# Exponentials of a pair attention, moved from ScalarE's table to a power on GpSimd

## The chip, the cores and the metric

The kernel runs on one core of a Trainium2 chip. The metric is the device time of one execution in microseconds (us). The engines of a core are named as in the profile: PE is TensorE (matmuls; PEld are its weight loads), DVE is VectorE, ACT is ScalarE, POOL is GpSimd, SP is SyncE, which here issues DMAs. Each engine takes its instructions in order.

## The reference

Two layers on x of 4 x 1024 x 256 in float32: a recurrent attention and a mixture of experts, then a pair attention and a feed-forward net with two hidden layers. The change lies in the pair attention alone. Cut to what matters, it computes for each batch:

```
q = X @ Wq.T ; k = X @ Wk.T ; Vy = X @ Wy_w.T + Wy_b      # 64 features a
e[i,j,a]    = relu(signed_sqrt(q[i,a] + k[j,a]))
scores[i,j] = sum_a e[i,j,a] * Wphi[a]
ex          = exp(scores - max_j scores)
denom       = sum_j ex
part1       = ex @ Vy
Ew[i,a]     = sum_j ex[i,j] * e[i,j,a]
out         = (part1 + Ew @ We_w.T + We_b * denom) / (denom + 1e-9)
```

The table e has 1024 x 1024 x 64 entries per batch, and it is used twice: for the scores, and, once the exponentials are known, for Ew.

## The kernel before

The first stage (to about 1300 us) is the first layer. The second stage runs the pair attention of all four batches, and interleaves with it the rest of the first layer (`first_rest`), the preparation of the next batch (`prepare`) and the feed-forward net (`dense`), cut into pieces that one function, `work(room)`, emits at fixed points. A list of allowances, `ROOM`, says how much of it goes in at each point. A few feed-forward pieces run on after the last block.

The pair attention is cut into blocks of 32 query rows, `NB` = 32 blocks a batch and 128 in all (class `Block`). A block has eight steps, each with one pair of tiles. The two halves of a pair tile (128 partitions, which hold 16 queries by 8 features, by 1024 keys) go through the same work:

- `pair` (L1313, L1315, L1316): adds the query to the spread keys and clips at zero, six of sixteen halves on ACT (L1313), ten on DVE (L1315); ACT takes the square root of the whole pair (L1316), and PE sums the features into the scores (L1320, PSUM tile `sc`).
- `top` (L1330 to L1333): DVE takes the maximum of each of the 128 rows of scores; a row of queries lies over four partitions, so a small matmul brings their maxima together.
- `exps` (L1337 to L1340): DVE takes the final maximum with its sign turned (`neg`); ACT makes `ex` from the scores, 128 x 256. At its end `switch()` emits a Silu or Gelu of the feed-forward net (L1290), if one is due, so that ACT's tables are changed at one place in a block.
- `spread` (L1345), twice a block: PE copies the exponentials of half of the queries to the partitions where the pair tiles have them (`xb`, in PSUM, 128 x 1024).
- `weigh` (L1364): DVE multiplies each half tile by `xb` and sums over the keys, 16 times a block.
- `turn` and `turned` (L1350, L1354): PE transposes `ex`, and ACT copies it out for the product with the values. `finish` (L1412 among its lines) completes four blocks at a time.

The order of the work is written out by hand in a loop over blocks n and steps p. At each step it weighs pair p of block n, emits some of the other work, and makes a pair that is 11 or 12 pairs ahead, as the ring of `RING` = 12 pair tiles allows. At p = 5 it emits `top` of block n + 1, and at p = 6 its `exps` and its first `spread`; the second `spread` follows at p = 0 of its own block. What DVE is given between `neg` and the first `weigh` that reads the new `xb` is thus the making of pairs at steps 6 and 7, the weighing of step 7 and pieces of the other work. On POOL there are only additions in this stage: `finish` (L1412), `dense` (L1278) and `first_rest` (L1095, L1165).

Of the kernel before, what the change touches and what calls it, by code (L numbers as in the profile page):

```python
# [7 lines left out]
F32 = mybir.dt.float32  # L8
AF = mybir.ActivationFunctionType
ALU = mybir.AluOpType  # L10
# [4 lines left out]
P = 128  # L15
# [7 lines left out]
CAP = 640.0  # L23
EPS_RHO = 1e-8
EPS_DEN = 1e-9
DFF = 1024
FB = 256
U = 512
# [12 lines left out]
@with_exitstack  # L41
def block_kernel(ctx: ExitStack, tc: tile.TileContext, a, out):
    nc = tc.nc
    keep = ctx.enter_context(tc.tile_pool(name="keep", bufs=1))


    kept = ctx.enter_context(tc.tile_pool(name="kept", bufs=1, space=DRAM))
    link = {
        "x1": [kept.tile([U, C], F32, tag=f"x1_{j}", name=f"x1_{j}") for j in range(B * T // U)],
        "x2": [kept.tile([FB, C], F32, tag=f"x2_{j}", name=f"x2_{j}") for j in range(B * T // FB)],  # L50
        "gates": [kept.tile([1, 2, B, C], F32, tag=f"gates{j}", name=f"gates{j}") for j in range(2)],
        "brow": kept.tile([1, C], F32, tag="brow", name="brow"),
        "yg": kept.tile([P, 4, U], F32, tag="yg", name="yg"),
        "qd": kept.tile([T, 64], F32, tag="qd0", name="qd0"),
        "kd": kept.tile([8, P, T], F32, tag="kd0", name="kd0"),
        "vd": kept.tile([T, C], F32, tag="vd0", name="vd0"),
    }

    ident = keep.tile([P, P], F32, tag="ident", name="ident")
    nc.scalar.dma_start(ident, a["ident"])  # L60
    eps = keep.tile([P, 3], F32, tag="eps", name="eps")
    for i, v in enumerate((EPS_LN, EPS_GN, EPS_RHO)):
        nc.vector.memset(eps[:, i : i + 1], v)
    cols = [keep.tile([P, 6, 2, B], F32, tag=f"mcols{i}", name=f"mcols{i}") for i in range(2)]
    seen = keep.tile([P, NE], F32, tag="seen", name="seen")
    nc.gpsimd.memset(seen, 0.0)
    first_layer(tc, a, link, cols, seen, ident, eps)
    pair_attention(tc, a, link, out, cols, seen, ident, eps)
# [733 lines left out]
def pair_attention(tc, a, link, out, cols_of, seen, ident, eps):  # L802
# [10 lines left out]
    nc = tc.nc  # L813
# [4 lines left out]
    with tc.tile_pool(name="at_w", bufs=1) as wp, tc.tile_pool(name="at_2", bufs=2) as p2, tc.tile_pool(  # L818
        name="at_k", bufs=1
    ) as pk, tc.tile_pool(name="at_s", bufs=RING) as ring, tc.tile_pool(  # L820
        name="at_d", bufs=2, space=DRAM
    ) as dr, tc.tile_pool(name="at_f", bufs=1) as pf, tc.tile_pool(name="at_fw", bufs=4) as pfw, tc.tile_pool(
        name="at_sc", bufs=2, space=PSUM
    ) as psc, tc.tile_pool(name="at_xb", bufs=2, space=PSUM) as pxb, tc.tile_pool(
        name="at_g", bufs=2, space=PSUM
# [10 lines left out]
        nc.vector.memset(wsel, 0.0)  # L836
        for g in range(8):
            nc.vector.tensor_scalar_mul(wsel[:, g, 16:32], query, phi[:, g : g + 1])
        same = wp.tile([P, P], F32, tag="same", name="same")
        part = wp.tile([P, 4], F32, tag="part", name="part")  # L840
        pick = wp.tile([P, 4, 2, P], F32, tag="pick", name="pick")
# [155 lines left out]
        def weights(j, i):  # L997
            for k in range(j * ALL + i, min(j * ALL + i + 3, B * T // FB * ALL)):
                if k not in held:
                    held[k] = pfw.tile([P, DFF], F32, tag="fw", name="fw")  # L1000
                    nc.sync.dma_start(held[k], a["ffw"][k % ALL * P : (k % ALL + 1) * P, :])
# [23 lines left out]
        def first_rest():  # L1025
# [6 lines left out]
            nc.sync.dma_start(x, a["x"][(NU - 1) * U :, :].rearrange("(t p) c -> p t c", p=P))  # L1032
            fw = [pfw.tile([P, DFF], F32, tag="fw", name="fw") for i in range(3)]
            wo, (center, avg, tri, ones) = fw[0][:, 0:512], (fw[0][:, 512 + P * i : 640 + P * i] for i in range(4))
# [113 lines left out]
            def half(n):  # L1148
                t = pfw.tile([P, DFF], F32, tag="fw", name="wd").rearrange("p (k n) -> p k n", k=2)
                i, k = divmod(n, 2)  # L1150
                nc.sync.dma_start(t, w_down[:, 2 * k : 2 * k + 2, 2 * i * C : 2 * (i + 1) * C])
                return t
# [141 lines left out]
        def switch():  # L1294
            while waiting:
                waiting.pop(0)()

        class Block:
# [36 lines left out]
            def exps(self):  # L1335
                self.neg = p2.tile([P, 1], F32, tag="neg", name="neg")
                nc.vector.tensor_reduce(self.neg, self.sc[:, 256:260], AX.X, ALU.max, negate=True)  # L1337
                self.ex = p2.tile([P, 256], F32, tag="ex", name="ex")
                nc.scalar.activation(self.ex, self.sc[:, 0:256], AF.Exp, bias=self.neg)  # L1339
                switch()  # L1340

            def spread(self, s):
# [25 lines left out]
        def finish(n, ew, exT):  # L1368
# [37 lines left out]
            den = p2.tile([P, 1], F32, tag="den", name="den")  # L1406
            nc.vector.tensor_scalar_add(den, o[:, C : C + 1], EPS_DEN)
            nc.vector.reciprocal(den, den)
# [120 lines left out]
def _arranged(inputs):  # L1529
# [21 lines left out]
    for n in "vg":  # L1551
# [13 lines left out]
    arr["ffw"] = np.concatenate(  # L1565
        [w[n].reshape(2, P, 2, 512).transpose(2, 1, 0, 3).reshape(2 * P, DFF) for n in ("w1", "w2")]
        + [w[n].reshape(8, P, 8, P).transpose(2, 1, 0, 3).reshape(8 * P, DFF) for n in ("h1", "h2")]
        + [w["w3"].reshape(2, 4, P, C).transpose(0, 2, 1, 3).reshape(2 * P, DFF)]
    )
# [21 lines left out]
```

## Time and profile before

| | |
|---|---|
| median of 3 runs | 5620.06 us (5608.47 to 5624.56) |
| the profiled execution's own time | 5612.39 us |
| its span, first to last instruction | 5610.4 us |
| mean granted TensorE clock | 0.884 |
| first and last exponential (L1339) | 1307.2 and 5386.9 us |
| ACT table loads at L1339 / L1316 / L1290 | 128 / 127 / 46, 1283 ns each |

The span is what the instruction records cover; the profiled execution's own time has about 2 us more around it. In the rows, a group of instructions shows busy time and the mean of one in ns; after the bar stand the idle time of its engine in front of it and what ended that. In the waits, each line has the engine and line that waited, what it waited for, the total in us, how many times, and the longest. In the timeline a line has a start in us, a duration, the engine and the instruction.

### The profile page before, as it was taken

What the parts mean: (1) busy time and instruction counts of PE and PEld (TensorE: products, weight loads), DVE (VectorE), ACT (ScalarE), POOL (GpSimd) and SP (SyncE); (2) the same over time, 40 slices, a digit from 0 to 9 for tenths busy, and PEclk for the clock granted to TensorE, in tenths of its full rate; (3) what the DMA queues carried; (4) which work ended last, traced back from release to release, by engine and by line L of the source; (5) the groups of instructions that cost most, each with busy time, mean ns of one, the idle gap of its engine ahead of it and who ended that gap; (6) DMA issues with size and microseconds to landing.
All of it is one profiled execution on the core that took longest, in us unless ns stands there. A gap on an engine that the chain in (4) does not pass through costs nothing.

```text
span 5610.4 us, 74442 instructions
## 1 busy us (share of the span) xinstructions
PE 4574.4 (82%) x28714; PEld 2695.6 (48%) x28714; DVE 4532.2 (81%) x7889; ACT 3854.0 (69%) x3550; POOL 534.3 (10%) x463
## 2 busy tenths in 40 slices
PE   6789888765778778888896788897888897888888
PEld 2233333332345445555463555564555564555566
DVE  5777777656888888889988788888889989898951
ACT  2322222117888888888887888888788888888840
POOL 3434433220000000000000000000000000000000
PEclk8789999886889889998898889898899898988999
DMA  4333333332011131211112221111211211111123
GB/s 133 100 94 94 95 89 97 102 95 68 25 36 47 38 70 61 82 61 57 45 69 46 60 82 59 51 63 34 71 53 60 87 65 44 57 56 50 44 95 115
DMA packets 223734, 385.48 MB, mean 69 GB/s; under 512 B 69346, under 2 KB 114963, under 8 KB 222995
## 3 DMA queue, kind: packets, MB, share of 16 engines
q1 hardware_dynamic: 211890, 378.46, 21.7%
q8 instruction: 226, 3.70, 0.3%
q10 hardware_dynamic: 11488, 2.25, 0.2%
q14 instruction: 130, 1.06, 0.1%
HBM read 340.74 MB, written 39.86 MB: 68 GB/s over the span
## 4 chain that ended last, share of the span: by engine, by line
PE 44%; DVE 31%; ACT 16%; SPq 4%; issue 3%; DMA 2%; POOL 0%; ACTq 0%; DVEq 0%; POOLq 0%
PE ff_ps L1249 14%; DVE s L1364 13%; PE sc L1320 8%; ACT s L1316 7%; DVE s L1315 5%; PE e_ps L591 5%; PE xb L1345 4%; DVE state L777 2%; ACT s L1313 2%; PE ff_ps L1226 2%; PE out_ps L1268 2%; ACT wide L1290 2%; ACT L1316 2%; DVE pr L779 2%; SPq L955 1%
## 5 line engine op out<-in xcount | busy, mean ns | idle before, releaser
L1364 DVE CUSTOM_DVE_ANT_0 s<-s,xb 128x1024 f32<-128x1024 f32 x2048 | 2412.6, 1215 | 37.7 <-PE xb L1345 36.5
L1316 ACT ACTIVATE s<-s,eps 128x2048 f32<-128x2048 f32 x1024 | 2039.0, 2001 | 379.3 <-DVE s L1315 362.3
L1320 PE MATMUL sc<-s,wsel 128*32 128x256 f32 x16384 | 1235.4, 427 | 727.2 <-ACT s L1316 725.8
L1320 PEld LDWEIGHTS sc<-s,wsel 128*32 128x32 f32 x16384 | 463.3, 117 | 1334.5 <-ACT s L1316 898.6
L1249 PE MATMUL ff_ps<-wide,fw 128*128 128x256 f32 x4096 | 983.5, 389 | 8.6 <-ACT wide L1290 8.5
L1315 DVE TENSOR_SCALAR s<-kB,qt 128x1024 f32<-128x1024 f32 x1280 | 947.3, 758 | 35.3 <-DMA wk<-in_Wk_dram 17.1
L1313 ACT ACTIVATE s<-kB,qt 128x1024 f32<-128x1024 f32 x768 | 875.0, 1139 | 102.7 <-DMA wk<-in_Wk_dram 59.1
L1249 PEld LDWEIGHTS ff_ps<-wide,fw 128*128 128x128 f32 x4096 | 769.2, 193 | 181.9 <-issue 74.5
L1345 PE MATMUL xb<-ex,pick 128*128 128x256 f32 x2048 | 591.6, 439 | 16.6 <-ACT ex L1339 15.8
L1345 PEld LDWEIGHTS xb<-ex,pick 128*128 128x128 f32 x2048 | 423.3, 218 | 208.1 <-issue 75.5
L591 PE MATMUL e_ps<-wd,hid 128*128 128x512 f32 x896 | 424.7, 621 | 0.0
L709 POOL TENSOR_TENSOR kv<-vb,out_k 128x512 f32<-128x512 f32 x256 | 323.7, 1272 | 332.4 <-DVE state L777 202.7
L777 DVE TENSOR_TENSOR_SCAN state<-dec,carry,kv 128x512 f32<-128x512 f32 x256 | 326.0, 1273 | 9.6 <-POOL carry L772 5.0
L1412 POOL TENSOR_TENSOR xr<-xr,fin 128x256 f32<-128x256 f32 x32 | 34.2, 1068 | 2877.8 <-DVE fin L1410 2650.4
L591 PEld LDWEIGHTS e_ps<-wd,hid 128*128 128x128 f32 x896 | 174.8, 201 | 245.0 <-issue 238.4
L779 DVE TENSOR_TENSOR pr<-state,rec 128x512 f32<-128x512 f32 x256 | 176.0, 687 | 110.8 <-ACT state L775 57.5
L1226 PE MATMUL ff_ps<-wide,fw 128*128 128x256 f32 x1024 | 255.5, 400 | 3.3 <-DVE wide L1213 1.5
L1238 DVE TENSOR_TENSOR wide<-ff_ps,ffn_s 128x512 f32<-128x512 f32 x128 | 88.1, 688 | 208.7 <-PE ff_ps L1249 207.7
L769 ACT COPY carry<-state 128x1 f32<-128x1 f32 x255 | 47.8, 188 | 271.4 <-DVE state L777 270.3
L1226 PEld LDWEIGHTS ff_ps<-wide,fw 128*128 128x128 f32 x1024 | 200.2, 201 | 50.1 <-issue 12.1
L1330 DVE TENSOR_REDUCE own<-sc 128x1 f32<-128x256 f32 x128 | 54.0, 422 | 170.6 <-PE sc L1320 170.6
L1364 DVE DVE_READ_ACCUMULATOR2_ANT ew<- 128x1 f32 x2048 | 168.7, 82 | 0.0
(247 smaller groups left out, 3879.9 us busy)
## 6 DMA issues: line engine op xcount, KB each, us to landing
fw<-in_ffw_dram SPq DMA_DIRECT2D x352, 512.0 KB
vb<-vd SPq DMA_DIRECT2D x1024, 64.0 KB
wd<-in_w_down_dram SPq DMA_DIRECT2D x28, 1024.0 KB
kB<-kd SPq DMA_DIRECT2D x32, 512.0 KB
kd<-wide SPq DMA_DIRECT2D x24, 512.0 KB
vd<-out_v SPq DMA_DIRECT2D x8, 512.0 KB
kd<-kn SPq DMA_DIRECT2D x16, 256.0 KB
vy<-vd SPq DMA_DIRECT2D x4, 1024.0 KB
```

The lines of the kernel that those rows point to most:

```text
L591: nc.tensor.matmul(ps, hid[:, k, t * P : (t + 1) * P], wd[:, k, :], start=k == 0, stop=k == HID // P - 1)
L709: nc.gpsimd.tensor_mul(kv, vb[:, g % 2, :], ready[u]["k"][:, n // HN, :])
L777: nc.vector.tensor_tensor_scan(s[:, 1 : U + 1], dec, kv, c, ALU.mult, ALU.add)
L779: nc.vector.tensor_mul(pr, s[:, 0:U], rec)
L1226: nc.tensor.matmul(ps[:, h, :], w[:, k, o : o + P], hT[:, k, :], start=k == 0, stop=k == 1)
L1249: nc.tensor.matmul(ps[:, h, :], w[:, k * P : (k + 1) * P], of[:, k, :], start=k == 0, stop=k == 7)
L1313: nc.scalar.activation(t[:, h, :], kB[self.b][g], AF.Relu, bias=q)
L1315: nc.vector.tensor_scalar(t[:, h, :], kB[self.b][g], q, 0.0, ALU.add, ALU.max)
L1316: nc.scalar.activation(t, t, AF.Sqrt, bias=eps_rho)
L1320: nc.tensor.matmul(self.sc[32 * j : 32 * j + 32, 0:256], wsel[:, g, 16 * (1 - s) : 16 * (1 - s) + 32], t[:, h, 256 * j : 256 * (j + 1)], s ...
L1345: nc.tensor.matmul(xb[:, 256 * j : 256 * (j + 1)], pick[:, j, s, :], self.ex, start=True, stop=True)
L1364: nc.vector.tensor_tensor_reduce(t[:, h, :], t[:, h, :], self.xb[s], 1.0, 0.0, ALU.mult, ALU.add, ew[:, self.n % 4, col : col + 1])
```

## The change

The new tile `euler` holds e, 2.718281828459045, once per partition, and is read as if it were 256 columns wide. ACT adds `neg` to the scores with Identity instead of Exp. GpSimd then computes euler to the power of `ex`, elementwise in float32, in place in `ex`. All readers of `ex` (both spreads and `turn`) take it from GpSimd now.

```diff
+EULER = 2.718281828459045
...
+        euler = wp.tile([P, 1], F32, tag="euler", name="euler")
+        nc.gpsimd.memset(euler, EULER)
+        euler = euler.to_broadcast([P, 256])
...
                 self.ex = p2.tile([P, 256], F32, tag="ex", name="ex")
-                nc.scalar.activation(self.ex, self.sc[:, 0:256], AF.Exp, bias=self.neg)
+                nc.scalar.activation(self.ex, self.sc[:, 0:256], AF.Identity, bias=self.neg)
+                nc.gpsimd.tensor_tensor(self.ex, euler, self.ex, ALU.pow)
                 switch()
```

## The prediction

> **What bounds the kernel now.** I read the page first (busy shares, slices, the chain), then the groups of instructions, the waits, and the timeline of one block.
>
> ```profile
> PE 4574.4 (82%) x28714; PEld 2695.6 (48%) x28714; DVE 4532.2 (81%) x7889; ACT 3854.0 (69%) x3550; POOL 534.3 (10%) x463
> ...
> POOL 3434433220000000000000000000000000000000
> ...
> PE 44%; DVE 31%; ACT 16%; SPq 4%; issue 3%; DMA 2%; POOL 0%; ACTq 0%; DVEq 0%; POOLq 0%
> PE ff_ps L1249 14%; DVE s L1364 13%; PE sc L1320 8%; ACT s L1316 7%; DVE s L1315 5%; PE e_ps L591 5%; PE xb L1345 4%; DVE state L777 2%; ACT s L1313 2%; PE ff_ps L1226 2%; PE out_ps L1268 2%; ACT wide L1290 2%; ACT L1316 2%; DVE pr L779 2%; SPq L955 1%
> ```
>
> The exponentials live in the stage from about 1304 to 5430 us. There POOL is idle (the zeros of its row from slice 11 on), while PE, DVE and ACT share the chain; a sum over that stage gives DVE 3602.75 us busy of 4126, ACT 3503.53, PE 3396.66. No engine bounds it alone; DVE comes nearest. In the chain, "ACT L1316" without a tile is table loads: 2%, about 112 us. Loads of L1339 are under the list's last 1%, so at most 56 us. The groups give the sizes:
>
> ```profile
> L1364 DVE CUSTOM_DVE_ANT_0 s<-s,xb 128x1024 f32<-128x1024 f32 x2048 | 2412.6, 1215 | 37.7 <-PE xb L1345 36.5 <-ACT wide L1290 0.4
> ...
> L1339 ACT ACT_TABLE_LOAD x128 | 164.2, 1283 | 2.3
> L1316 ACT ACT_TABLE_LOAD x127 | 162.9, 1283 | 3.8 <-DVE s L1315 1.5
> ...
> L1339 ACT ACTIVATE ex<-sc,neg 128x256 f32<-128x256 f32 x128 | 60.7, 474 | 24.1 <-DVE neg L1337 22.8
> ...
> L1412 POOL TENSOR_TENSOR xr<-xr,fin 128x256 f32<-128x256 f32 x32 | 34.2, 1068 | 2877.8 <-DVE fin L1410 2650.4 <-DMA xr<-x 186.8 <-DVE ln_rs L895 40.7
> ```
>
> The waits say what late ACT work costs the others:
>
> ```profile
> PE sc L1320 <- ACT s L1316: 685.3, 360, 25.9
> ...
> DVE own L1330 <- PE sc L1320: 170.6, 43, 31.0
> ...
> DVE s L1364 <- PE xb L1345: 36.5, 49, 2.3
> ```
>
> PE waits much for square roots, but only what reaches DVE counts: 170.6 us in front of the row maximum (L1330). Last, one block's exponential in the timeline (start, duration):
>
> ```profile
> 3027.42 0.16 DVE L1337 TENSOR_REDUCE neg<-sc 128x1 f32<-128x4 f32 x1 [1.34 <-PE sc L1333]
> 3027.43 1.28 ACT L1339 ACT_TABLE_LOAD   x1
> ...
> 3028.73 0.47 ACT L1339 ACTIVATE ex<-sc,neg 128x256 f32<-128x256 f32 x1
> ...
> 3030.15 1.99 PE L1345 MATMUL xb<-ex,pick 128*128 128x256 f32 x8
> ...
> 3030.56 1.42 DVE L1315 TENSOR_SCALAR s<-kB,qt 128x1024 f32<-128x1024 f32 x2
> ...
> 3032.18 1.22 DVE L1364 CUSTOM_DVE_ANT_0 s<-s,xb 128x1024 f32<-128x1024 f32 x1 [0.20 <-PE xb L1345]
> ```
>
> This is the place that decides. After `neg` DVE has work of its own until 3031.98, 4.40 us from neg's end at 3027.58; a block near 3055 gives 4.45. Then it needs `xb`, which needs `ex`. The two paths are even: the idle time on xb is only 36.5 us over 128 blocks, 0.29 us each.
>
> **The change, part by part.**
>
> Removed on ACT: L1339's 128 loads, 164.2 us, and the square root's reload after them. L1290 still loads for Silu or Gelu 46 times, directly after an exponential, and a reload follows each; so about 127 - 46 = 81 of L1316's loads go, 104 us. Together 268 us of ACT. That Identity needs no load is in the trace: L909, Identity, ran at 3004.48 between square roots at 3002.57 and 3006.55 with no load. What of the 268 is on the path? The chain allows 112 + 56 = 168 us at most, the wait at L1330 170.6; I take 170 as the whole gain there. A rule bears on this. A load shows 1.28 us, and the timeline has the activation 1.30 us after the load's start, with the square root in front ending at 3027.41. The Trainium skill, "ScalarE: Activation LUTs", What ACT_TABLE_LOAD costs, adds a drain for about 2.66 us in all. By it ACT would be freed of 209 x 2.66 = 556 us instead of 268. The rows decide: 268.
>
> Kept: one ACT pass of 0.474 us (L1339, now Identity; same form). The `euler` memset is once, 0.1 us like the other small POOL memsets, under the loads at the stage's start: nothing.
>
> Added: 128 POOL instructions, 128x256, one per block, each in series between ACT's subtraction and PE's L1345. Call its duration X. The trace shows no power. From below, the nearest row is L1412, an addition of the same shape: 0.73 us when undisturbed, 1.07 mean. [...]a power is a logarithm, a product and an exponential[...], so arithmetic, not reading, should set X and that row is only a floor. From above I use a price. The Trainium skill, "GPSIMD Engine Reference", Performance pitfalls for Q7 kernels, puts a chain of dependent fp32 operations at 4 cycles per element each, at the 1.2 GHz of its Specifications: 256 columns x 4 / 1.2 = 853 ns per step of the chain. How many steps is my assumption: ScalarE's exp is three multiply-adds over a finely cut table (first page named, Cubic eval); without the table I double that, six for the exponential, six for the logarithm, one product: 13 steps, 11.1 us, and 0.2 us fixed (POOL additions of 1024 and 512 columns, 2348 and 1272 ns, extrapolate to 0.2): X = 11.3 us. With independent chains interleaved it could be near 3 us; with twice the steps and range handling near 30. I keep 0.73 as the lower end and 30 as the upper end of this form.
>
> The path after neg becomes 0.47 + X + 1.99 (L1345) + four handovers of about 0.05 (0.04 from xb to L1364 above) = X + 2.66 us. DVE's cover is 4.40. Stall X - 1.74, of which 0.29 is there already: X - 2.0 more per block, 9.3 us at X = 11.3. Over the 127 gaps between blocks: +1181 us. PE stands too: it issues in order, the two L1345 groups' first waits for `ex`, and behind it are the feed-forward matmuls (L1226, L1249), the scores (L1320) and all else, so it cannot use the stall. ACT can catch up with its backlog of square roots and then runs dry, as L1315's results stop; the 170 us gain is therefore the most that comes back.
>
> The second rule speaks against the change. DVE's L1315 takes 0.75 us for 1024 columns, and against a POOL instruction it stretches:
>
> ```profile
> 1624.21 1.88 DVE L1315 TENSOR_SCALAR s<-kB,qt 128x1024 f32<-128x1024 f32 x2
> 1624.37 1.17 POOL L1165 TENSOR_TENSOR wide<-wide,wide 128x256 f32<-128x256 f32 x1 [0.64 <-DVE wide L1164]
> ```
>
> Two of them took 1.88 us where 1.42 is usual, and POOL 1.17 where 0.73 is its best. The Trainium skill, "SBUF — State Buffer", Who interferes with whom, calls this an exclusive lock held for the whole instruction. By the rule, the L1315 pair of the last step (up to 1.42 us) waits for the entire power; by the row's 0.46 us alone it would lose half a microsecond. Either way the pair then runs beside L1345's 1.99 us, before xb is complete: cost nothing on DVE. If that cover failed it would be 127 x 1.42 = 180 us, kept for the range. POOL may in turn wait up to 0.75 us for a running L1315: inside the bounds of X.
>
> Queues: on POOL the power stands behind the additions L1412 and L1278, which wait for DVE results issued before neg. Twice L1412 waited last for its DMA, so a few late landings are possible: tens of us at most. No DMA is moved; the `xr` and output stores behind POOL may come up to X later, with several blocks until their readers.
>
> Sum: the profiled execution took 5612.39 us; +1181 - 170 gives about 6623. The median of the runs is 7.7 us higher: 6630 us.
>
> **Rivals.**
>
> 1. Faster: the power is near the addition's price. Up to X = 1.74 the stall vanishes, and the gain is 170.6 plus the 36.5 of xb, at most 207; two thirds of it give 5480. It decides at 127 x (X - 2.0) = 170, X = 3.3 us: below that the change wins. For it: the L1412 row[...]. Against it: 3.3 us leaves (3.3 - 0.2) x 1200 / 256 = 14.5 cycles per column, under four dependent steps.
> 2. The power is done value by value, not 16 lanes at once[...]: 16 x 11.1 = 178 us, 127 x 176 more, about 28,000 us, with every engine idle most of the time. No POOL row here looks like that, but none is such an operation.
> 3. The loads are not gone (Identity or another function loads again): 170 us come not back, 6800. L909 speaks against it.
>
> **How the numbers follow.** A measurement of this kernel tells about 0.3% from no change. Forecast (X from 3.5 to 30): 0.70; rival 3: 0.02; rival 2: 0.13; rival 1: 0.13; X so near 3.3 that nothing shows: 0.02. Faster 0.13, same 0.02, slower 0.85. The likeliest case's own range is 5640 to 9010 (X = 30: 127 x 28 - 170 = +3390). The range takes in the cheap power, 5415 (5620 - 207), and leaves out rival 2: 5415 to 9010.
>
> **What would show it.** In the profile after: no load at L1339, about 46 at L1316; 128 POOL rows whose mean is X; DVE's L1364 waiting for xb X - 1.7 us a block, PE's L1345 waiting for POOL; ACT's share falling by more than its 268 us over the longer span; the span growing by 127 x (X - 2.0) less some 170. If X is large and xb is not waited for, my cover is wrong; if X is under 3.3 us, the step that sized the power failed.

## The result, and the profile after

The kernel after takes 10626.34 us (three runs, 10623.29 to 10627.13) against 5620.06 us before: a ratio of 1.892, 95% interval 1.8885 to 1.8955. The sign was forecast, the size was not: 6630 us was predicted, at most 9010. The profiled execution has a span of 10624.5 us. All added lines shift the numbering: L1339 is now L1343, the power is L1344, L1345 is L1350, L1364 is L1369, L1315 and L1316 are L1319 and L1320, L1330 is L1334, L1412 is L1417.

Busy times and two rows of slices of the page after, with the clock's row of the page before below them:

```profile
PE 4718.9 (44%) x28714; PEld 2788.9 (26%) x28714; DVE 4533.6 (43%) x7889; ACT 3596.3 (34%) x3337; POOL 5817.0 (55%) x592
...
POOL 4333255566556555655665566556655655565551
PEclk7888766666666666666666666666666666666678
```

```profile
PEclk8789999886889889998898889898899898988999
```

DVE did the same work as before in microseconds (4533.6 against 4532.2) in 1.9 times the span. ACT is 258 us lighter, near the 268 us of the removed loads. POOL is full for 5 or 6 tenths of every slice of the stage, and the granted TensorE clock, which was at 8 or 9 tenths in nearly all of the stage before, is at 6. The groups and the loads left on ACT:

```profile
L1344 POOL TENSOR_TENSOR ex<-euler,ex 128x256 f32<-128x256 f32 x128 | 5282.3, 41268 | 3257.7 <-ACT ex L1343 3202.2
L1369 DVE CUSTOM_DVE_ANT_0 s<-s,xb 128x1024 f32<-128x1024 f32 x2048 | 2411.4, 1214 | 5259.0 <-PE xb L1350 5259.0
L1350 PE MATMUL xb<-ex,pick 128*128 128x256 f32 x2048 | 734.1, 520 | 5123.4 <-POOL ex L1344 5123.4
```

```profile
L1320 ACT ACT_TABLE_LOAD x46 | 59.0, 1283 | 2.3 <-DVE s L1319 1.5
L1294 ACT ACT_TABLE_LOAD x46 | 59.0, 1283 | 84.6 <-DVE wide L1242 70.0 <-DVE wide L1211 13.8
```

The power takes 41.27 us, not 11.3. What it costs is one number: DVE waits 5259.0 us for `xb`, 36.5 before. The loads went as forecast: the 128 at the exponential are gone, and 81 of the 127 at the square root. One block in the timeline, to be held against the block of before:

```profile
5043.90 0.15 DVE L1341 TENSOR_REDUCE neg<-sc 128x1 f32<-128x4 f32 x1
5044.15 0.47 ACT L1343 ACTIVATE ex<-sc,neg 128x256 f32<-128x256 f32 x1 [0.35 <-DVE neg L1341]
...
5044.70 41.13 POOL L1344 TENSOR_TENSOR ex<-euler,ex 128x256 f32<-128x256 f32 x1 [19.00 <-ACT ex L1343]
...
5047.00 0.72 DVE L1319 TENSOR_SCALAR s<-kB,qt 128x1024 f32<-128x1024 f32 x1
...
5050.85 1.41 DVE L1319 TENSOR_SCALAR s<-kB,qt 128x1024 f32<-128x1024 f32 x2
...
5085.88 3.06 PEld L1350 LDWEIGHTS xb<-ex,pick 128*128 128x128 f32 x8 [40.97 <-POOL ex L1344]
5085.88 3.78 PE L1350 MATMUL xb<-ex,pick 128*128 128x256 f32 x8 [40.09 <-POOL ex L1344]
...
5089.70 1.22 DVE L1369 CUSTOM_DVE_ANT_0 s<-s,xb 128x1024 f32<-128x1024 f32 x1 [37.44 <-PE xb L1350]
```

Three things to see. The chain neg, subtraction, power, spread, weighing is the one that was foreseen. The spread behind the power takes 3.78 us where 1.99 had been read off. And L1319 runs at its usual pace in the middle of a power. In this block DVE has some 7 us of work behind `neg`, because pieces of the other work (L894, L906) fall into it; the mean wait of the 128 blocks is 41.1 us.

### The profile page after: what moved, and what is told of

The parts are those of the page before. It is cut to its first block, busy times and chain, and to the rows that moved or that the text cites. A ratio compares the mean times of both kernels' runs of the same rounds, so it can differ in the third digit from the quotient of the medians.

```text
span 10624.5 us, 74464 instructions
## 1 busy us (share of the span) xinstructions
PE 4718.9 (44%) x28714; PEld 2788.9 (26%) x28714; DVE 4533.6 (43%) x7889; ACT 3596.3 (34%) x3337; POOL 5817.0 (55%) x592
## 5 line engine op out<-in xcount | busy, mean ns | idle before, releaser
L1344 POOL TENSOR_TENSOR ex<-euler,ex 128x256 f32<-128x256 f32 x128 | 5282.3, 41268 | 3257.7 <-ACT ex L1343 3202.2
L1369 DVE CUSTOM_DVE_ANT_0 s<-s,xb 128x1024 f32<-128x1024 f32 x2048 | 2411.4, 1214 | 5259.0 <-PE xb L1350 5259.0
L1350 PE MATMUL xb<-ex,pick 128*128 128x256 f32 x2048 | 734.1, 520 | 5123.4 <-POOL ex L1344 5123.4
L1320 ACT ACTIVATE s<-s,eps 128x2048 f32<-128x2048 f32 x1024 | 2045.8, 2002 | 854.4 <-DVE s L1319 837.0
L1350 PEld LDWEIGHTS xb<-ex,pick 128*128 128x128 f32 x2048 | 507.1, 260 | 5346.7 <-POOL ex L1344 5204.3
L1319 DVE TENSOR_SCALAR s<-kB,qt 128x1024 f32<-128x1024 f32 x1280 | 946.9, 757 | 33.8 <-DMA qt<-qd 15.6
L1282 POOL TENSOR_TENSOR res<-res,wide 128x512 f32<-128x512 f32 x16 | 24.7, 1543 | 422.6 <-DVE wide L1281 422.6
L913 ACT ACTIVATE wide<-ln_ps,mcols 128x256 f32<-128x256 f32 x60 | 30.4, 557 | 637.0 <-PE ln_ps L910 637.0
L1417 POOL TENSOR_TENSOR xr<-xr,fin 128x256 f32<-128x256 f32 x32 | 35.2, 1099 | 245.8 <-DVE fin L1415 231.2
L1369 DVE DVE_READ_ACCUMULATOR2_ANT ew<- 128x1 f32 x2048 | 167.0, 82 | 0.0
```

The source lines that it names most:

```text
L1319: nc.vector.tensor_scalar(t[:, h, :], kB[self.b][g], q, 0.0, ALU.add, ALU.max)
L1320: nc.scalar.activation(t, t, AF.Sqrt, bias=eps_rho)
L1344: nc.gpsimd.tensor_tensor(self.ex, euler, self.ex, ALU.pow)
L1350: nc.tensor.matmul(xb[:, 256 * j : 256 * (j + 1)], pick[:, j, s, :], self.ex, start=True, stop=True)
L1369: nc.vector.tensor_tensor_reduce(t[:, h, :], t[:, h, :], self.xb[s], 1.0, 0.0, ALU.mult, ALU.add, ew[:, self.n % 4, col : col + 1])
```

## The experiments

The theory put to the test: the time follows from the power's place in the path, about 127 us for each microsecond of its duration, plus a part for the slower TensorE clock; ScalarE's relief is worth what DVE had waited for. The rivals: another part of the change costs (contention between POOL and DVE, the queue on POOL), the stall is filled by other work, or the duration is a set-up that has nothing to do with the columns. Times are medians with the ratio to the kernel before on the same chip.

### The gain alone

```diff
-                nc.gpsimd.tensor_tensor(self.ex, euler, self.ex, ALU.pow)
```

> The power is left out: ex holds the scores less their maximum, as ScalarE's Identity writes them, and goes on to both spreads and the transpose; all else is as after the change. This is the change's gain alone (209 table loads fewer, no GpSimd in the path). Theory (path: what comes back is what DVE waited for late square roots at the row maximum, 170.6 us, and for xb, 36.5 us): 5413 us, ratio to before 0.963. Rival (ScalarE's loads were hidden; PE and DVE set the pace in any case): within 0.5% of before, 5600 to 5640 us. Second rival (all 268 us of ScalarE come back): 5350 us. No table loads at the exponential's line, 46 to 48 at the square root's.

5504.62 us, ratio 0.9797 (0.9774 to 0.9819): 112 us less. It lies between theory and first rival. DVE's waits in the pair attention, from ahead of its first row maximum to its last weighing (1285 to 5413 us before, 1282 to 5298 us here), first before, then here (L1242, L1281 and L1217 are L1238, L1277 and L1213 of the kernel before; L1368 and L1349 are L1369 and L1350 of the kernel after):

```profile
DVE wide L1238 <- PE ff_ps L1249: 96.7, 45, 6.7
DVE wide L1277 <- PE out_ps L1268: 81.6, 13, 6.8
DVE wide L1213 <- PE ff_ps L1226: 36.8, 28, 3.4
```

```profile
DVE own L1334 <- PE sc L1324: 157.8, 43, 30.2
DVE wide L1242 <- PE ff_ps L1253: 77.0, 32, 5.0
DVE wide L1281 <- PE out_ps L1272: 45.6, 14, 4.5
DVE s L1368 <- PE xb L1349: 39.2, 47, 3.3
DVE wide L1217 <- PE ff_ps L1230: 6.9, 14, 0.8
```

The wait at the row maximum, where the gain was expected, went only from 170.6 to 157.8 us, and that at xb not at all. What shrank are the three waits for the feed-forward matmuls, from 215.1 to 129.5 us together. All of DVE's waits in this stretch fell from 494 to 386 us, and these 108 us are the gain. PE itself waited less for square roots (725.8 us before, 665.6 here, over the whole run), so ScalarE's relief seems to reach DVE by way of PE; that step is argued from these rows, no run tests it. Part of the freed ACT time turned into ACT waiting for DVE, 427.0 us at the square root against 362.3.

### A cheap operation in the power's place

```diff
-                nc.gpsimd.tensor_tensor(self.ex, euler, self.ex, ALU.pow)
+                nc.gpsimd.tensor_tensor(self.ex, euler, self.ex, ALU.mult)
```

> A multiplication of the same shape stands in the power's place on GpSimd (the exponential is thus left out); same waits, X about 0.73 to 1.2 us. Theory (DVE's cover after neg is 4.40 us, the path X + 2.66 us, so nothing stalls below X = 1.74): as identity_only within 0.5%. Rival (there is no such cover: any instruction between ScalarE and the spread is paid in full, about 1.1 us in each of 127 gaps): 140 us above identity_only.

5505.35 us, ratio 0.9796 (0.9770 to 0.9822): as without it. The multiplication took 760 ns in the mean, and DVE waited 40.1 us for xb. The detour over GpSimd costs nothing by itself; DVE's work after neg covers it.

### The power on 16 and on 64 columns

```diff
-                nc.gpsimd.tensor_tensor(self.ex, euler, self.ex, ALU.pow)
+                nc.gpsimd.tensor_tensor(self.ex[:, 0:16], euler[:, 0:16], self.ex[:, 0:16], ALU.pow)
```

> The power runs on the first 16 of 256 columns only; the other 240 keep the difference. If the power's time goes by columns (41.12 us / 256 = 161 ns each), X is 2.6 to 2.8 us. Theory: 127 x (X - 1.74) = about 135 us above identity_only, about 5550 us. Rival (the power has a large fixed part, a library set-up or a loading of code, of tens of us): X stays above 20 us and the time above 8000 us. Rival (no cover): 127 x 2.7 = 340 us above identity_only.

5713.59 us, ratio 1.0167 (1.0144 to 1.0190), 209 us above the run without it: more than the 135 expected. A block's first spread takes 2.98 us in the mean here, against 2.62 us in the run without the power.

```profile
L1369 DVE CUSTOM_DVE_ANT_0 s<-s,xb 128x1024 f32<-128x1024 f32 x2048 | 2411.3, 1214 | 305.2 <-PE xb L1350 305.2
...
L1344 POOL TENSOR_TENSOR ex<-euler,ex 128x16 f32<-128x16 f32 x128 | 422.2, 3298 | 3259.8 <-ACT ex L1343 3203.2 <-issue 56.7
```

The same with 64 in place of 16:

> The power runs on the first 64 of 256 columns, near the 11.3 us that the prediction took for the whole: X 10.3 to 10.5 us. Theory: 127 x (X - 1.74) = 1100 us above identity_only, near 6520 us; with the slower TensorE clock after a wait up to 180 us more. Rival (the stall is partly filled by PE's or ScalarE's other work): 6000 us or less. It tests the sum of the prediction at the duration that it assumed.

6727.77 us, ratio 1.1971 (1.1944 to 1.1997), 1223 us above the run without it.

```profile
L1369 DVE CUSTOM_DVE_ANT_0 s<-s,xb 128x1024 f32<-128x1024 f32 x2048 | 2411.3, 1214 | 1345.1 <-PE xb L1350 1345.1
...
L1344 POOL TENSOR_TENSOR ex<-euler,ex 128x64 f32<-128x64 f32 x128 | 1366.4, 10675 | 3270.8 <-ACT ex L1343 3215.6 <-issue 55.2
```

From 64 columns to all 256 the time rises by 3899 us over 30.59 us of duration: 127.4 us for each microsecond, one gap between blocks each. No other work fills the stall, as PE, which would have to do it, stands in it too. Divided by the 128 blocks, DVE's wait for xb is 2.4, 10.5 and 41.1 us at durations of 3.30, 10.68 and 41.27: at the short one 0.9 us of the duration is hidden, at the long ones 0.2, where the prediction hid 1.74. The first spread explains the order: 2.98, 3.74 and 3.73 us in the mean.

### What the power's duration depends on

On top of the kernel before, behind its last output, with tiles of their own (two of each):

```diff
+        for i in range(2):
+            nc.gpsimd.tensor_tensor(po[:, 0:256], e1[:, 0:256], px[:, 0:256], ALU.pow)
...
```

> The kernel before (Exp on ScalarE), and after its last output GpSimd alone runs powers on tiles of its own, twice each: 128 x 256, 128 x 128, 128 x 512, 128 x 256 with all exponents 0, with exponents a hundred times as large (many results infinite or 0), 16, 8 and 1 partitions x 256, 128 x 256 with a full tile as the base instead of a broadcast column, and the multiplication. Theory (16 lanes in step, one chain of steps for each column, no branch on the data): about 159 ns a column plus a fixed part under 1 us, so 41, 21 and 82 us; the same 41 us for any exponents, for 16, 8 and 1 partitions and for the full base. Rival (value by value, one core's 16 partitions in turn): 8 partitions take half of 16, and 1 partition a sixteenth, about 3 us. Rival (steps that depend on the data): zeros and overflows shorten or lengthen it by 10% or more. Multiplication 0.73 us.

POOL in the timeline at the end of this run, in the order of the list above:

```profile
5605.83 82.37 POOL L1507 TENSOR_TENSOR po<-euler,pin 128x256 f32<-128x256 f32 x2 [3.01 <-DMA pin<-in_x_dram]
5688.28 41.51 POOL L1509 TENSOR_TENSOR po<-euler,pin 128x128 f32<-128x128 f32 x2
5729.87 163.91 POOL L1511 TENSOR_TENSOR po<-euler,pin 128x512 f32<-128x512 f32 x2
5893.85 82.31 POOL L1513 TENSOR_TENSOR po<-euler,pin 128x256 f32<-128x256 f32 x2
5976.24 82.31 POOL L1515 TENSOR_TENSOR po<-euler,pin 128x256 f32<-128x256 f32 x2
6058.63 82.29 POOL L1517 TENSOR_TENSOR po<-euler,pin 16x256 f32<-16x256 f32 x2
6140.99 82.29 POOL L1519 TENSOR_TENSOR po<-euler,pin 8x256 f32<-8x256 f32 x2
6223.36 82.29 POOL L1521 TENSOR_TENSOR po<-euler,pin 1x256 f32<-1x256 f32 x2
6305.73 82.53 POOL L1523 TENSOR_TENSOR po<-pin 128x256 f32<-128x256 f32 x2
6388.33 1.30 POOL L1525 TENSOR_TENSOR po<-euler,pin 128x256 f32<-128x256 f32 x2
```

Each row is two instructions, and their durations are what is read from this run. Between 128 and 512 columns, (163.91 - 41.51) / 2 / 384 gives 159.4 ns a column, and 0.35 us is left as fixed. Exponents of zero (L1513) or a hundred times as large (L1515), a full tile as base (L1523) and one partition instead of 128 (L1521) change it by less than 0.3%. Both rivals fall, for the exponents tried and the one base: the duration follows the columns, not the partitions and not the data.

### The clock behind the wait

```diff
                 xb = pxb.tile([P, T], F32, tag="xb", name="xb")
+                if s == 0:
+                    for i in range(76):
+                        nc.tensor.matmul(self.sc[:, 260:512], ident, pick[:, 0:2].rearrange("p j s m -> p (j s m)")[:, 0:252], start=True, stop=True)
```

> The kernel after, whole power in the path; in front of a block's first spread PE runs 76 matmuls of 252 columns on constant tiles into an unused part of the scores' bank, about 36 us at full clock, so that it works while the power runs. Theory (the wait lets TensorE's clock sink, and the first spread after it takes 3.78 us instead of 1.99): the first spread at 2.0 to 2.4 us, and the time 127 x 1.4 to 1.8 = 180 to 230 us below the kernel after, about 10420 us. Rival (the spread is slow for another reason, such as loading its code or its weights after a long wait): spread still near 3.8 us and no gain. Rival (the matmuls outlast the power at a lower clock): slower than the kernel after.

10627.74 us, ratio 1.8919 (1.8891 to 1.8947): no gain. The matmuls ended early, as PE's rows show:

```profile
5043.76 34.49 PE L1351 MATMUL sc<-pick,ident 128*128 128x252 f32 x152
5083.92 3.78 PE L1353 MATMUL xb<-ex,pick 128*128 128x256 f32 x8 [5.67 <-POOL ex L1344]
```

A gap of 5.67 us remained, and the spread was as slow as behind 40 us. So either the gap is long enough, or idleness is not the reason. The next run tells them apart, with 88 matmuls in place of 76:

> As pe_kept_busy, with 88 matmuls instead of 76, so that PE works nearly until the power ends (76 took 34.5 us and left a gap of 5.7 us, after which the spread still took 3.78 us). Theory (a gap of some 6 us is enough to halve TensorE's pace for the next 5.5 us): spread at 2.0 us, time 180 to 230 us below the kernel after, about 10410 us. Rival (the pace after the wait has to do with the wait itself, not with idleness): spread still 3.78 us, time within 0.3% of the kernel after, 10630 us. If the 88 outlast the power by a microsecond or two, up to 250 us are lost instead.

10435.38 us, ratio 1.8557 (1.8515 to 1.8600): 191 us below the kernel after.

```profile
5016.33 2.98 PE L1353 MATMUL xb<-ex,pick 128*128 128x256 f32 x8 [3.36 <-POOL ex L1344]
...
5045.77 37.67 PE L1351 MATMUL sc<-pick,ident 128*128 128x252 f32 x176
5085.02 1.99 PE L1353 MATMUL xb<-ex,pick 128*128 128x256 f32 x8 [1.59 <-POOL ex L1344]
```

The granted clock in the spread, here and in the kernel after (the last figure but two of a row):

```profile
5085.02:5087.01 1.99, 1.99 (x9) 1.50 (x10) 0.00 (x0) 0.00 (x0) 0.00 (x0) 1.00 0.00 0
5085.88:5089.66 3.78, 3.78 (x12) 2.59 (x16) 0.00 (x0) 0.00 (x0) 0.00 (x0) 0.50 0.00 0
```

Behind a gap of 1.59 us the spread takes 1.99 us at a clock of 1.00, behind 3.36 us 2.98 at 0.64, behind 5.67 us 3.78 at 0.50. The power was as long as before (41269 ns), and DVE's wait for xb fell from 5259.0 to 5080.2 us. The clock's part of the loss is shown: about 190 us of 5006.

The three rows are single blocks. Over all 128 of this run, the 76 gaps of up to 1.93 us left a spread of 1.99 us each, while 22 of the 28 between 2.05 and 2.28 us were followed by a slower one, of up to 3.68 us; all 128 gaps of the run with 76 matmuls, 5.51 us and longer, gave 3.40 to 3.78. The Trainium skill, "TensorE: Matmul & The Clock Gate", Part 1, has TensorE fall to half its clock after an idle window of about 3.4 us. The half clock is there, but by that figure gaps of 2.05 us should have been free; here the measurement decides. (The ends of matmuls are modelled in the profile, so the gaps are not exact.)

### A power beside the path

ScalarE keeps Exp and its loads; GpSimd takes a power of half the columns into a tile that nobody reads:

```diff
-                nc.scalar.activation(self.ex, self.sc[:, 0:256], AF.Identity, bias=self.neg)
-                nc.gpsimd.tensor_tensor(self.ex, euler, self.ex, ALU.pow)
+                nc.scalar.activation(self.ex, self.sc[:, 0:256], AF.Exp, bias=self.neg)
+                aside = p2.tile([P, 128], F32, tag="aside", name="aside")
+                nc.gpsimd.tensor_tensor(aside, euler[:, 0:128], self.ex[:, 0:128], ALU.pow)
```

> The kernel before with Exp on ScalarE and all table loads; beside it GpSimd takes the power of 128 of the exponential's columns into a tile that nobody reads: some 20.7 us of GpSimd in each block of 32, off the path. Theory (only the place in the path costs; DVE's L1319 ran at its usual 0.75 us inside powers in the profile after): within 0.5% of before. Rival (exclusive lock of the port that DVE and GpSimd share, held for the whole power): ten DVE instructions a block must get by it, many wait up to 20 us: thousands of us slower. Middle: the lock held only while data is read or written, up to 1.5 us a block, 190 us slower.

5723.48 us, ratio 1.0182 (1.0163 to 1.0200): 104 us slower, more than the theory allowed and far from thousands. From its timeline:

```profile
3038.14 20.73 POOL L1345 TENSOR_TENSOR aside<-euler,ex 128x128 f32<-128x128 f32 x1 [20.19 <-ACT ex L1343]
3039.38 0.72 DVE L1319 TENSOR_SCALAR s<-kB,qt 128x1024 f32<-128x1024 f32 x1
3043.23 1.41 DVE L1319 TENSOR_SCALAR s<-kB,qt 128x1024 f32<-128x1024 f32 x2
...
3047.49 0.75 DVE L1319 TENSOR_SCALAR s<-kB,qt 128x1024 f32<-128x1024 f32 x1
```

```profile
L1315 DVE TENSOR_SCALAR s<-kB,qt 128x1024 f32<-128x1024 f32 x1280 | 947.3, 758 | 35.3 <-DMA wk<-in_Wk_dram 17.1
L1319 DVE TENSOR_SCALAR s<-kB,qt 128x1024 f32<-128x1024 f32 x1280 | 945.8, 756 | 33.6 <-DMA we<-in_We_dram 15.4
```

DVE's L1319 is not held: 756 ns in the mean of 1280 in the second row (758 before, the first), under a POOL that is busy 65% of the stage; the 865 that lie wholly inside a power have a mean of 751 ns. DVE's busy time in the stage is the same too (3597.94 us against 3602.75), so the 104 us are idle time. POOL's additions now stand behind powers. The next run takes them out of that queue:

```diff
-            nc.gpsimd.tensor_add(xr, xr, fin)
+            nc.vector.tensor_add(xr, xr, fin)
...
```

> As exp_kept_pow_aside (104 us slower than before), with the stage's additions L1099, L1169, L1282 and L1418 moved from GpSimd to DVE, so that none of them stands behind a 20.7 us power. They cost DVE about 32 x 0.42 + 16 x 0.69 + 4 x 0.42 + 2 x 0.69 = 27 us. Theory (the 104 us come from these additions waiting up to 20.7 us in GpSimd's queue, and their readers with them): about 5645 us, 25 us above before. Rival (contention with the running power, for instance for SBUF): about 5750 us, as exp_kept_pow_aside plus 27 us.

5666.72 us, ratio 1.0085 (1.0062 to 1.0109): 46 us above before. The additions cost DVE some 27 us of that by their rows (13.6 for the 32 of `finish`, 11.1 for the 16 of `dense`, the rest for six others, estimated from the same rates). DVE's busy time in the stage rose by 21 us. So the queue explains about 80 to 85 of the 104 us. DVE's waits bear this out in part: that at the row maximum went from 197.1 us with the additions behind powers to 156.4 without, that for x from DRAM (L894) from 45.5 to 16.4. Those for the feed-forward matmuls (136.9 and 133.1 us at L1242, 96.7 before) and for xb (57.3 and 58.2, 36.5 before) stayed up; what causes them, and the 20 us or so that remain, stay open.

### The loads kept beside a stall

pow64 with `AF.Exp` instead of `AF.Identity`:

> As pow64, but ScalarE keeps Exp, with its table loads (the power then works on the first 64 columns of the exponentials, so the result of those columns is another). It tells whether the 112 us that the removed loads bring without the power are still worth as much beside the stall. Additive: 6728 + 112 = 6840 us, with the loads' 1.28 us in front of the power in the path up to 6728 + 163 = 6891 us. Rival (ScalarE's loads hide in the stall): 6730 to 6750 us, so the gain of the change is nothing once it stalls.

6876.26 us, ratio 1.2240 (1.2219 to 1.2260): 148 us above pow64. The loads do not hide in the stall. DVE's wait for xb is 1485.7 us against 1345.1: the load in front of the exponential lies in the same path as the power, 1.1 us in each gap. So a gain from the removed loads survives beside a stall of this length; in the kernel after it would be small against the power.

## Why the prediction was wrong, step by step

- **What bounds the kernel**: right. The place named, DVE between neg and xb, took the whole loss: the wait grew by 5222 us, and about 216 us came back elsewhere (5620 + 5222 - 10626).
- **The power's duration X**: this step failed. "How many steps is my assumption: 13 steps, 11.1 us" gave X = 11.3 us; measured 41.27. The term is short by 30 us x 127 = 3806 us of the 3996 by which the forecast missed; with 41.27 in its own sum the prediction comes to 10437 us, 189 below the result. At the 4 cycles that the Trainium skill, "GPSIMD Engine Reference", Performance pitfalls for Q7 kernels, gives for each operation of a dependent chain, and its 1.2 GHz, the measured 159.4 ns a column would be 48 steps: an estimate, since no run shows the steps. The upper end of 30 us was drawn from the same guess, twice the steps, and so the range failed with it. The shape was right (by columns, not by partitions, small fixed part); the number was not to be had from the trace before. A rule that gives the price of a step bounds nothing while the number of steps is free.
- **The sum 127 x X**: right, 127.4 us for each microsecond between 64 and 256 columns.
- **The path behind the power**: "Stall X - 1.74" was too small, by the term for the spread. DVE's cover of 4.40 us held: in the mean of the 128 blocks its work between `neg` and the wait for xb was 4.64 us before and 4.75 after. The spread's 1.99 us was read from one block at full clock; in the mean a block's first spread took 2.54 us before and 3.73 after. DVE's wait for xb grew by 5222 us, where the sum with the measured X gives 4987: 235 us more. Keeping PE at work until 1.6 us before the spread returned 191 us; the first attempt, with a gap of 5.7 us, returned nothing.
- **The gain**: "I take 170" was too high for the loads alone (112 us, shown), and it was read from the wrong wait. Of the 170.6 us at the row maximum 157.8 stayed when the loads were gone; 85.6 us came back at the waits for the feed-forward matmuls. In the kernel after, all of DVE's waits but that for xb fell from 458 to 262 us, by 196 of the 216 us; this holds the gain and what else the stall let catch up, and the two were not taken apart.
- **Contention**: cost nothing, as forecast, but for another reason. The rule of an exclusive lock for the whole instruction did not hold for the power: in the kernel after, the 251 of L1319 that lie wholly inside a power took 751 ns in the mean. No cover was needed.
- **Queues on POOL**: "tens of us at most" for additions in front of the power. What the runs showed is the reverse case, additions behind a power, about 80 to 85 us with a power of 20.7 us aside. In the kernel after that share was not measured by itself.
- **The rivals**: the cheap power was wrong by X alone; at 0.76 us in its place the gain was 112 us, not 140. The power value by value is excluded by the probes, where one partition takes as long as 128. The loads were gone. The point from which the change decides lies, by 127 us for each microsecond back from pow16, at about 2.5 us (an estimate), not 3.3.

No run that computes the exponentials was faster than the kernel before. The runs bound what a replacement could have brought: even with nothing in the power's place the time is 5504.62 us, 2.0% below before, and the replacement would have to take under about 2.5 us.

## What to carry to other kernels

When an operation is moved to an engine on which the trace has never shown it, its duration is the forecast: measure that one instruction on idle tiles first (a pair of each shape settles columns, lanes and data), and if that is not possible, let the range reach as far as the ignorance does. Price the neighbours of a new wait by what they take behind a wait, not by what they take in a running stream. And do not take the largest wait on a late engine for the gain of relieving it: here 268 us of ScalarE were worth 112, and most of it came back at other waits. To see where, compare waits between the same two points of both kernels.

## What the runs showed of the hardware that was not expected

- A float32 power on GpSimd takes 159.4 ns a column plus 0.35 us, with exponents of 0, of the input and of a hundred times the input, and for 1 to 128 partitions; the multiplication of 128x256 took 0.65 us there, 63 times less.
- A running power does not hold up DVE's L1319, while an addition does. In the same profile after, with an addition (L1169) beside a pair of L1319, the pair takes 1.88 us instead of 1.41:

```profile
2029.76 1.88 DVE L1319 TENSOR_SCALAR s<-kB,qt 128x1024 f32<-128x1024 f32 x2
2029.92 1.17 POOL L1169 TENSOR_TENSOR wide<-wide,wide 128x256 f32<-128x256 f32 x1 [0.64 <-DVE wide L1168]
```

  The Trainium skill, "SBUF — State Buffer", Who interferes with whom, says that the lock is held for the whole instruction; for the power the measurement decides against it. Why was not tried.
- TensorE's granted clock fell from 1.00 to 0.50 behind short gaps: none of the 76 gaps of up to 1.93 us slowed the spread behind it, 22 of the 28 from 2.05 to 2.28 us did, and behind 5.51 us or more all did. In the block shown of the kernel after, the clock stayed at 0.50 until about 4.7 us after the spread had begun.
